# Zero-weight matmuls between the steps of a selective scan, and sums over states issued in odd units

## The chip, the cores and the metric

The kernel runs on one core of a Trainium2 chip. The metric is the device time of one execution in microseconds, and the time given is the median of the runs made. The engines of the core are named as in the profile: PE (TensorE), DVE (VectorE), ACT (ScalarE), POOL (GpSimd) and SP (SyncE, which here only issues DMAs).

## What is computed

Four layers work on 4 images of 64 x 64 positions with 128 channels. Layers 0 and 1 hold a two-dimensional selective scan; layer 2 is a gated message between neighbouring positions, layer 3 a 7 x 7 neighbourhood attention. The change lies in the scan of layers 0 and 1, whose core is, for each of four directions k, each inner channel d and each of 16 states n:

```python
def step(h, t):
    x_t, d_t, B_t, C_t = t
    h = jnp.exp(d_t[..., None] * A) * h + (d_t * x_t)[..., None] * B_t[:, :, None, :]
    return (h, jnp.einsum('bkdn,bkn->bkd', h, C_t))
_, ys_l = jax.lax.scan(step, h0, scan_in)
```

The scan runs over 4096 positions, along rows or along columns of the image, forwards or backwards. Around it stand projections, a 3 x 3 depthwise convolution, normalisations, gates and, in layer 1, an MLP. Layer 0 has 128 inner channels, layer 1 has 256.

## The kernel before

**Stages.** A short start; then one long scan stage for layers 0 and 1 together (about 200 to 11,487 us of the profiled span); then layers 2 and 3. The change touches the scan stage, and a constant at the start.

**Units.** A task is one image and one tile of 128 inner channels: 4 tasks in layer 0, 8 in layer 1. A task has 4 directions x 4 steps of 1024 positions x 16 units = 256 units, so there are 3072 units in all. A unit is 8 channels x 16 states on the 128 partitions, 1024 positions long. Two units make a pair, which shares one tile h.

**What a pair goes through.** A DMA on SP's queue brings delta times x into h, repeated over the states (`Scans.load`, L440), 10 units ahead. DVE multiplies both halves by B (`times`, L446). For each unit PE spreads delta over the states with two bf16 matmuls into a PSUM tile da (`decay`, L454), ACT turns da into exp(A delta) in place (L456), and DVE scans (`scan`, L465). da has two buffers, so the matmuls of unit u+2, issued in unit u, wait for the scan of unit u. ACT saves the last state (`save`, L483), POOL multiplies the pair by C (L446 again), and PE adds it over the states with four float32 matmuls into the PSUM tile yps (`add_up`, L547). Each float32 matmul shows as two records in the trace, so the sums of a pair are 8 records. yps is opened every 8 units by `sum_so_far` (L522 or L530, a matmul of the input or of the y of earlier directions) and copied out by ACT after 8 units (`keep`, L557). The tile h has 9 buffers; the load of pair p+9 waits for the sums of pair p.

**The order.** It is written out by hand in `Scans.run`: one turn of its loop is one unit, and each engine executes its instructions in the order in which the turns issue them. With v = u - LAG and LAG = 4, sums are issued in even units: those of pair p in unit 2p + 6. The order of a turn is: scan(u); in odd units the product with B; in even units save and the product with C; decay(u+2); add_up; keep; sum_so_far; then the pieces of other work; then load(u+10).

**The other work.** `prepare` (delta, B and C of later steps) and `Side` (everything else of layers 0 and 1) are generators cut into small pieces, each with a hint of the engines that it uses. Their recorded instructions stand under L97, since they go through the helper `Counted`. `Plan.slot` keeps an estimated time for PE, ACT and POOL, with 3.6 us for a unit, and is told how much of a unit's PE time the sums take: `1.6 * even`. A piece is issued in a unit if the estimate says that it fits. Its PE results go through one PSUM bank, ms. Its stores are posted and flushed to SP's queue later.

Of the kernel before, what the change touches and what calls it, by code (L numbers as in the profile page):

```python
# [10 lines left out]
BF16 = mybir.dt.bfloat16  # L11
# [6 lines left out]
P = 128  # L18
# [3 lines left out]
T = 512  # L22
# [22 lines left out]
class Consts:  # L45


    def __init__(self, tc, pool, d_gather, d_spread):
        nc = tc.nc

        gather = pool.tile([P, 56], F32, name="gather")
        nc.sync.dma_start(out=gather, in_=d_gather)
        self.gather = [gather[:, 24 - 8 * jj : 56 - 8 * jj] for jj in range(4)]

        self.spread = pool.tile([96, 4, P], BF16, name="spread")
        with tc.tile_pool(name="spread32", bufs=1) as tmp:
            spread = tmp.tile([96, 4, P], F32, name="spread32")
            nc.sync.dma_start(out=spread, in_=d_spread)
            nc.vector.tensor_copy(self.spread, spread)
        self.ident = pool.tile([P, P], F32, name="ident")  # L60
        make_identity(nc, self.ident)
        self.ones128 = pool.tile([P, P], F32, name="ones128")
        nc.vector.memset(self.ones128, 1.0 / 128.0)
        self.cen128 = pool.tile([P, P], F32, name="cen128")
        nc.vector.tensor_sub(self.cen128, self.ident, self.ones128)
        self.cen256 = pool.tile([P, P], F32, name="cen256")
        self.neg256 = pool.tile([P, P], F32, name="neg256")
        nc.vector.memset(self.neg256, -1.0 / 256.0)
        nc.vector.tensor_add(self.cen256, self.ident, self.neg256)
        self.eps = pool.tile([P, 1], F32, name="eps")  # L70
        nc.vector.memset(self.eps, EPS)
# [202 lines left out]
NU = ND * NSTEP * NG  # L274
AHEAD = 28
LEAD = 10
LAG = 4


class Scans:  # L280
# [253 lines left out]
    def add_up(self, p):  # L534

        hc = self.live.pop(("h", p))
        for v in range(2):
            t, step, jj, j, g = self.unit(2 * p + v)
            for i in range(HALVES):
# [6 lines left out]
                    out = out.rearrange("p (r l) -> p r l", l=ROWS)  # L546
                self.nc.tensor.matmul(out, self.C.gather[jj], rhs, start=False, stop=jj == 3)  # L547

    def keep(self, u):

        nc = self.nc
        t, step, jj, j, g = self.unit(u)
        k, c = t.steps[step]
        b = u % NG // 8
        if step == 0 and b == 0:
            t.y = self.pool.tile([P, L], F32, name="y", tag="y", bufs=1)
        nc.scalar.copy(self.part(t.y, k, c, b), self.like_part(self.live.pop("yps"), k))  # L557
        if step < len(t.steps) - 1:
            return
        for i in range(HALVES):  # L560
            for v in range(2):
                at, to = i * H + 32 * v, b * H + 32 * v
                src = t.y[at : at + 32, b * L // 2 : (b + 1) * L // 2].rearrange("p (a x) -> p a x", x=T)
                dst = t.yd[to : to + 32, :].rearrange("p (a i x) -> p a i x", i=HALVES, x=T)[:, :, i, :]
                self.later.append(lambda src=src, dst=dst: nc.sync.dma_start(out=dst, in_=src))

    def run(self, between):

        total = NU * len(self.tasks)
        first = self.tasks[0]  # L570
        first.W.load()
        for _ in self.fetch(first):
            pass
        for _ in self.prepare(first, 0):
            pass
        self.plan.start()
        pieces, fetch, fetched = Lane(self.plan, "prep", iter(())), iter(()), 0
        for u in range(-12, total + LAG + 1):
            v = u - LAG
            if 0 <= u < total:  # L580
                self.scan(u)
            if u % 2 and -1 <= u < total - 1:
                self.times(self.nc.vector, (u + 1) // 2, "B")
            if 0 < u <= total and u % 2 == 0:
                self.save(u // 2 - 1)
                self.times(self.nc.gpsimd, u // 2 - 1, "C")
            if 0 <= u + 2 < total:
                self.decay(u + 2)
                if (u + 2) % NG == 0:
                    self.bring_b(u + 2)  # L590
            if v > 0 and v % 2 == 0:
                self.add_up(v // 2 - 1)
            if v > 0 and v % 8 == 0:
                self.keep(v - 1)
            if 0 < v < total and v % 8 == 1:
                self.sum_so_far(v - 1)
            if u >= total:
                continue
            even, first_one = u % 2 == 0, u % NG == NG - 2
            self.plan.slot(  # L600
                u, 1.6 * even + 1.0 * (v % 8 == 1) + 2.0 * first_one, 0.25 * even + 0.7 * (v % 8 == 0)
            )
            ahead, rest = divmod(u + AHEAD, NG)
            if rest == 0:
                while pieces.step():
                    pass
                self.plan.flush("prep", "rep")
            if rest == 0 and 0 < ahead < total // NG:
                n, step = divmod(ahead, NU // NG)
                if step == 0 and self.tasks[n].W is not self.tasks[n - 1].W:  # L610
                    self.tasks[n].W.load()
                if step == 0 and fetched < n:
                    fetch, fetched = self.fetch(self.tasks[n]), n
                    for _ in range(self.tasks[n].W.nct):
                        next(fetch, None)
                pieces = Lane(self.plan, "prep", self.prepare(self.tasks[n], step))

            n, step = divmod(ahead + 1, NU // NG)
            if step == 0 and fetched < n < len(self.tasks) and self.tasks[n - 1].x_done:
                fetch, fetched = self.fetch(self.tasks[n]), n  # L620
            next(fetch, None)
            while (pieces.count < rest - 4 or pieces.fits()) and pieces.step():
                pass
            if u >= 0:
                n, i = divmod(u, NU)
                if self.later:
                    self.later.pop(0)()
                between(n, i)
            if 0 <= u + LEAD < total:
                self.load(u + LEAD)  # L630
        while self.later:
            self.later.pop(0)()
# [525 lines left out]
def scan_layers(tc, C, nb, x_in, d0, s0, d1, s1, out):  # L1158

    nc = tc.nc  # L1160
    with ExitStack() as es:
# [24 lines left out]
        def between(n, i):  # L1186
# [3 lines left out]

            done = group[n] - (1 if i >= 8 + LAG or n and group[n - 1] == group[n] else 2)
            left, rate = -(lane.count if lane else 0), 0.0
# [435 lines left out]
def layer2(tc, C, nb, x_in, x_out, d_w, d_rel, d_v, beside):  # L1628
    with ExitStack() as es:
# [11 lines left out]

        with tc.manual_schedule():
            run(statistics(0, range(8)))
            E.roots([E.rstd])
            run(project(0, range(4)))
            beside()

# [24 lines left out]
            third, second, last = halves[-3:]  # L1672
            gates = E.gates(out, last[2], [third[2]["var"]], [])
            run(merged(gates, E.finish(*third) + E.outputs(*second)))
            run(E.gather(*last, alone=True))
            E.roots([second[2]["var"]])
# [509 lines left out]
```

## Time and profile before

| | us |
|---|---|
| median of 3 runs (13,754.66 to 13,772.11) | 13,754.89 |
| the profiled execution | 13,747.0 |
| its span | 13,745.1 |
| busy in the span: PE / DVE / ACT / POOL | 9945.1 / 11,718.9 / 7914.9 / 9719.0 |
| granted TensorE clock, mean over the span | 0.744 |
| DMA moved | 2474.88 MB |

The page lists for each group of instructions its line, engine, operation, output and inputs with their shapes, its count, then busy time, mean length of one in ns, and the idle time of the engine just before with what ended it. A wait "A <- B" means that engine A stood idle at that line until B was done. In tables by stretch the columns are the busy time and count of PE, PEld (weight loads), DVE, ACT and POOL, then the granted clock as a share of full speed, the busy share of the DMA engines, and GB/s.

### The profile page before, as it was taken

How to read it: one execution, taken by the hardware profiler on the slowest of the kernel's cores; microseconds unless marked ns; L12 is line 12 of the kernel's file. 1: busy time of each engine (PE TensorE's matmuls, PEld its weight loads, DVE VectorE, ACT ScalarE, POOL GpSimd, SP SyncE). 2: the span in 40 equal slices, each digit the busy share in tenths (PEclk: the TensorE clock that was granted, in tenths of full speed). 3: DMA queues.
4: the chain of work that ended last, by engine and by line, in shares of the span. 5: the costliest groups of instructions: out<-in, count | busy, mean ns of one | idle time of the engine just before them, and what ended most of it. 6: DMA issues, size and time to landing. Idle time of an engine off the chain costs nothing. (4 is left out here: it accounts for less than half of the span.)

```text
span 13745.1 us, 120368 instructions
## 1 busy us (share of the span) xinstructions
PE 9945.1 (72%) x37178; PEld 2503.4 (18%) x37178; DVE 11718.9 (85%) x6980; ACT 7914.9 (58%) x10594; POOL 9719.0 (71%) x3218
## 2 busy tenths in 40 slices
PE   5777777777777777677776777777777766666688
PEld 1111111111111111111111111111111111111455
DVE  4998989989999889989999999999999993577555
ACT  3665556655665556555665555555555554655577
POOL 3777778877787778878887888888888884355200
PEclk7766766777677767767677777777777776778899
DMA  5878887898788878898889877878787873234300
GB/s 155 213 202 216 215 202 197 221 225 205 192 222 201 208 202 206 213 215 215 195 217 214 220 193 192 201 192 204 196 195 198 192 187 98 68 95 109 73 20 17
DMA packets 877051, 2474.88 MB, mean 180 GB/s; under 512 B 142456, under 2 KB 164096, under 8 KB 868216
## 3 DMA queue, kind: packets, MB, share of 16 engines
q1 hardware_dynamic: 876407, 2467.18, 72.6%
q8 instruction: 297, 4.87, 0.2%
q14 instruction: 347, 2.83, 0.1%
HBM read 2043.34 MB, written 272.37 MB: 168 GB/s over the span
## 5 line engine op out<-in xcount | busy, mean ns | idle before, releaser
L446 POOL TENSOR_TENSOR h<-h,repC 128x2048 f32<-128x2048 f32 x1536 | 6951.4, 4530 | 1708.5 <-ACT state L483 1370.7
L465 DVE TENSOR_TENSOR_SCAN h<-da,state,h 128x1024 f32<-128x1024 f32 x2304 | 5319.1, 2340 | 519.9 <-ACT da L456 401.5
L456 ACT ACTIVATE da<-da,av 128x1024 f32<-128x1024 f32 x3072 | 3338.7, 1088 | 3123.3 <-PE da L454 3106.0
L454 PE MATMUL da<-dp,spread 96*128 96x512 bf16 x6144 | 2481.8, 496 | 2302.3 <-DVE h L465 2275.6
L446 DVE TENSOR_TENSOR h<-h,B 128x2048 f32<-128x2048 f32 x1536 | 3476.9, 2264 | 363.7 <-DMA h<-dud 190.4
L547 PE MATMUL yps<-h,gather 128*32 128x512 f32 x12288 | 2424.3, 874 | 3.2 <-POOL h L446 3.2
L465 DVE TENSOR_TENSOR_SCAN h<-da,h 128x1024 f32<-128x1024 f32 x768 | 1727.6, 2281 | 160.8 <-ACT da L456 123.2
L454 PEld LDWEIGHTS <-spread 96*128 96x128 bf16 x6144 | 541.3, 107 | 5522.2 <-issue 5103.6
L97 PE MATMUL ms<-d,wts 128*128 128x512 f32 (+3 forms) x900 | 678.1, 878 | 213.2 <-POOL d L97 84.1
L97 ACT ACT_TABLE_LOAD x600 | 769.8, 1283 | 17.9 <-DMA h<-dud 2.6
L97 PE MATMUL ms<-xd,xpdt 8*128 8x512 f32 (+1 forms) x768 | 599.2, 870 | 220.7 <-ACT delta L97 71.9
L97 POOL TENSOR_TENSOR delta<-delta,low 128x1024 f32<-128x1024 f32 x192 | 452.3, 2356 | 382.0 <-ACT low L97 299.0
L1897 POOL COPY wide_total<-total 128x128 f32<-128x128 f32 x128 | 37.9, 296 | 830.1 <-DVE total L1895 642.7
L97 ACT CAST parts<-delta 128x1024 bf16<-128x1024 f32 x384 | 400.8, 1044 | 350.3 <-POOL delta L97 326.4
L530 PE MATMUL yps<-y,ident 128*128 128x512 f32 x576 | 508.2, 972 | 75.3 <-ACT y L557 73.3
L97 ACT ACTIVATE low<-ms,av 128x512 f32<-128x512 f32 x384 | 263.8, 687 | 451.0 <-PE ms L97 435.3
L97 POOL TENSOR_TENSOR low<-delta,xc 128x1024 f32<-128x1024 f32 x192 | 502.8, 2619 | 8.9
L547 PEld LDWEIGHTS yps<-h,gather 128*32 128x32 f32 x12288 | 281.7, 127 | 1089.4 <-issue 846.3
L97 PE MATMUL ms<-pad,diag 96*32 96x504 f32 (+1 forms) x2304 | 398.9, 801 | 108.8 <-DMA pad<-xid 80.5
L1453 ACT ACTIVATE hid<-hid,relb 128x1024 f32<-128x1024 f32 x288 | 322.8, 1146 | 265.8 <-DVE hid L1448 265.6
L1866 ACT ACTIVATE s<-s,least 128x512 f32<-128x512 f32 x512 | 372.3, 727 | 177.4 <-DVE least L1853 177.4
L1853 DVE CUSTOM_DVE_ANT_0 s<-sps,bias 128x512 f32<-128x512 f32 x512 | 323.3, 687 | 171.8 <-PE sps L1842 165.6
(284 smaller groups left out, 11039.2 us busy)
## 6 DMA issues: line engine op xcount, KB each, us to landing
h<-dud SPq DMA_DIRECT2D x3072, 512.0 KB
dp<-parts SPq DMA_DIRECT2D x2304, 64.0 KB
repC<-xdd SPq DMA_DIRECT2D x192, 512.0 KB
dud<-low SPq DMA_DIRECT2D x192, 512.0 KB
spread<-gd SPq DMA_DIRECT2D x72, 1024.0 KB
pad<-xid SPq DMA_DIRECT2D x192, 256.0 KB
szd<-o SPq DMA_DIRECT2D x96, 256.0 KB
xcd<-o SPq DMA_DIRECT2D x96, 256.0 KB
```

The costliest lines, as they stand in the source:

```text
L97: return call(*args, **kw)
L446: engine.tensor_mul(pair, pair, t.prepared[step][name].unsqueeze(1).to_broadcast([P, 2, TS]))
L454: self.nc.tensor.matmul(da[:, cols], self.C.spread[:, jj, :], dp[:, j, cols], start=True, stop=True)
L456: self.nc.scalar.activation(da, da, AF.Exp, scale=t.W.a[:, at : at + 1])
L465: nc.vector.tensor_tensor_scan(h[:, way], da[:, way], h[:, way], 0.0 if step % NSTEP == 0 else t.states[step - 1][:, u % NG : u % NG + 1], ...
L530: self.nc.tensor.matmul(self.like_part(yps, k), self.C.ident, self.part(t.y, k, c, b), start=True, stop=False)
L547: self.nc.tensor.matmul(out, self.C.gather[jj], rhs, start=False, stop=jj == 3)
L1453: nc.scalar.activation(hid, hid, AF.Gelu, bias=self.relb[:, m, t : t + 1])
L1853: self.nc.vector.tensor_tensor_reduce(out=self.live["s", n][:, h, :], in0=self.live["sps", n][:, h, :], in1=self.bias[case][:, h, :], scal ...
L1866: self.nc.scalar.activation(s, s, AF.Exp, scale=-1.0, bias=self.live["least", n][:, h : h + 1], accum_out=self.live["total", n][:, h : h + 1],
L1897: nc.gpsimd.tensor_copy(wide, total.unsqueeze(2).to_broadcast([P, self.NH, self.HD]))
```

## The change

`Consts` gets a 128 x 128 bf16 tile of zeros and a 128 x 512 bf16 tile of ones. At the end of each unit, after the other work's pieces and before load(u+10), two matmuls (even units) or three (odd units) multiply the ones by the zeros and add the result into the open yps; they are left out in the unit in which yps has just been copied out. LAG goes from 4 to 5, so that add_up, keep and sum_so_far are issued one unit later: the sums of pair p in unit 2p + 7. The plan is told the new place of the sums.

```diff
+        self.nothing = pool.tile([P, P], BF16, name="nothing")
+        nc.vector.memset(self.nothing, 0.0)
+        self.ones16 = pool.tile([P, T], BF16, name="ones16")
+        nc.vector.memset(self.ones16, 1.0)
...
-LAG = 4
+LAG = 5
...
+    def stay_busy(self, times):
+
+        for _ in range(times if "yps" in self.live else 0):
+            self.nc.tensor.matmul(
+                self.live["yps"], self.C.nothing, self.C.ones16, start=False, stop=False, skip_group_check=True
+            )
...
             self.plan.slot(
-                u, 1.6 * even + 1.0 * (v % 8 == 1) + 2.0 * first_one, 0.25 * even + 0.7 * (v % 8 == 0)
+                u, 1.6 * (not even) + 1.0 * (v % 8 == 1) + 2.0 * first_one, 0.25 * even + 0.7 * (v % 8 == 0)
             )
...
                 between(n, i)
+            self.stay_busy(3 if u % 2 else 2)
             if 0 <= u + LEAD < total:
                 self.load(u + LEAD)
```

## The prediction

> **What bounds the kernel now.** I began with the table of stages. The scan stage runs from 200 to 11,487 us, 82% of the span; columns are PE, PEld, DVE, ACT and POOL busy, granted clock, DMA share, GB/s.
>
> ```profile
> 200.00:11487.00 11287.00, 8218.74 (x26324) 1716.23 (x26328) 10418.23 (x4620) 6469.33 (x8005) 9062.68 (x2734) 0.72 0.83 204
> ```
>
> VectorE is busy 10,418 of 11,287 us (92%). PE is at 73% with a clock of only 0.72. Next the groups: all of VectorE's stage is scans and products with B.
>
> ```profile
> L465 DVE TENSOR_TENSOR_SCAN h<-da,state,h 128x1024 f32<-128x1024 f32 x2304 | 5319.1, 2340 | 519.9 <-ACT da L456 401.5
> L454 PE MATMUL da<-dp,spread 96*128 96x512 bf16 x6144 | 2481.8, 496 | 2302.3 <-DVE h L465 2275.6
> ```
>
> Then the waits: engine, line, what it waited for, total us, times, longest.
>
> ```profile
> PE da L454 <- DVE h L465: 2275.6, 1194, 10.6
> DVE h L465 <- ACT da L456: 524.7, 428, 10.4
> SPq L440 <- PE yps L547: 2652.2, 633, 11.5
> ```
>
> So VectorE loses 525 us waiting for exp(da), in 428 of 3072 units. That chain is: scan u-2 ends and frees the da bank, two matmuls on PE, one exp of 1.09 us on ACT, scan u. The timeline shows its room (PE rows, start, length):
>
> ```profile
> 5003.06 1.01 PE L454 MATMUL da<-dp,spread 96*128 96x512 bf16 x2 [3.56 <-DVE h L465]
> 5004.00 1.93 PE L547 MATMUL yps<-h,gather 128*32 128x512 f32 x8
> 5005.87 1.03 PE L454 MATMUL da<-dp,spread 96*128 96x512 bf16 x2
> 5009.81 1.01 PE L454 MATMUL da<-dp,spread 96*128 96x512 bf16 x2 [2.91 <-DVE h L465]
> ```
>
> VectorE's order is scan, scan, product B (2.34, 2.34, 2.26). So PE's da matmuls are released 2.3 us apart, then 4.6 us apart. Today the sums of y (1.93 us cold) sit in the short gap. The second da follows directly behind them, late; in the long gap PE idles 2.91 us. Between a bank's release and its next scan lie 4.6 us; 1.01 + 1.09 us of work and 0.2 of handing on leave 2.3 us of slack.
>
> Last, the clock. It is granted in windows of 3.41 us and is 0.50 or 1.00. Rows of such windows (length, PE busy, clock, DMA share, GB/s):
>
> ```profile
> 5027.90:5031.32 3.42, 3.42 (x10) 0.50 1.05 322
> 5031.32:5034.73 3.41, 2.74 (x15) 1.00 1.04 317
> 5034.73:5038.14 3.41, 1.57 (x8) 1.00 1.04 261
> 5038.14:5041.56 3.42, 0.62 (x2) 0.50 1.04 256
> 5041.56:5044.97 3.41, 3.07 (x11) 0.50 1.03 257
> 5044.97:5048.38 3.41, 2.54 (x6) 0.50 0.92 293
> ```
>
> A full cold window is followed by a warm one. A warm window at 80% keeps it, one at 46% loses it, and 90% of a cold window does not win it. I counted all 3306 windows of the stage so. Of 1453 warm ones, these stay warm: busy under 0.4, 0 of 346; 0.4 to 0.5, 4 of 126; 0.5 to 0.6, 84 of 138; 0.6 to 0.8, 296 of 396; above, 440 of 447; in all 57%. Of 1853 cold ones, these turn warm: under 0.8, 0 of 648; 0.8 to 0.9, 8 of 248; above, 621 of 957; in all 34%. In balance the warm share is 0.34/(0.34 + 0.43) = 0.44, clock 0.72, as the row says.
>
> **The change: fillers.** In the built program 6507 matmuls are added: two in even units, three in odd ones, none in the unit where the sum is copied out; 2.12 per unit. Nearest row: da, the same shape but 96 rows. A pair takes 0.60 us warm and 1.03 cold, one alone 0.38 and 0.6, so a further one is 0.215 warm and 0.43 cold. Their weight loads (0.1 us for da's) hide under the matmul before, as da's do; uncovered they would be 0.2 us of PE per unit. So a unit gets 0.46 us warm or 0.91 cold.
>
> What of it is hidden: PE idles 2276 us for scans, 0.74 us per unit, just where the fillers stand (directly ahead of the next da). A unit whose PE is on time pays nothing. A unit whose PE is late pays all of it, since da is queued behind. I followed each scan gap over 0.2 us back along its releasers. They sum to about 530 us; about 145 of them come through PE matmuls of the side work or the sums directly (some 220 us), about 180 through ACT, which had earlier waited for PE (some 218 us), and the rest from ACT, POOL or DMA. Bounds: 145 x 0.63 = +91 us, 325 x 0.63 = +205 us (0.63 at the clock worked out next). I take +91: in the second group the idle time often lies between.
>
> **The clock.** 0.46 us of 3.6 is +0.13 of a warm window, 0.91 of 3.68 is +0.25 of a cold one. Moving the counts by that much: warm windows of 0.3 to 0.4 (158) keep it in 0.1 of cases, 0.4 to 0.5 in 0.65, 0.5 to 0.6 in 0.75, 0.6 to 0.8 in 0.87, above as now: 16 + 82 + 104 + 345 + 440 = 987 of 1453, 68%. Cold windows above 0.7 (1353 in number with these at 0.7 to 0.8) become full, 70% of them turn; with 30 others 977 of 1853, 53%. Balance: 0.53/(0.53 + 0.32) = 0.62, clock 0.81; with the sums moved into the long gap I take 0.82 in the stage, 0.83 over the run (0.744 before).
>
> Here a rule of the Trainium skill is weighed (TensorE: Matmul & The Clock Gate, part 1, the clock gate): the clock falls after an idle window of about 3.4 us and comes after a busy one, so gaps under some 3 us are safe. By it, a PE with fillers in every gap would be warm nearly always, clock near 1. The rows above say otherwise: windows with 46% of work fall too, and 30% of even the full cold ones stay cold. The measurement decides: 0.82. The rule's end is a rival below.
>
> What is the clock worth? In the stage VectorE's busy time is its progress. By the table of 500 us stretches (same columns as the first row):
>
> ```profile
> 1000.00:1500.00 500.00, 372.62 (x1237) 70.83 (x1240) 443.96 (x198) 305.80 (x359) 379.12 (x119) 0.69 0.85 215
> 3500.00:4000.00 500.00, 362.65 (x1038) 74.94 (x1036) 456.36 (x202) 300.52 (x372) 402.40 (x120) 0.69 0.82 202
> 6000.00:6500.00 500.00, 380.94 (x1365) 72.72 (x1358) 458.27 (x204) 271.69 (x338) 397.89 (x119) 0.76 0.87 213
> 8000.00:8500.00 500.00, 362.98 (x1138) 80.69 (x1137) 475.82 (x212) 276.67 (x352) 425.96 (x129) 0.76 0.80 194
> ```
>
> The five full stretches at 0.69 average 457 us of VectorE, the twelve at 0.73 to 0.76 (mean 0.743) 464 us: 1.6% for 0.053. For +0.10 that is 3.0% of 11,287, 340 us. Cause runs both ways, since a stalled PE also cools. The lower bound is 0. I take two thirds, -227 us, because the direct working agrees: da (1.03 to 0.60), sums (1.93 to 1.07) and side matmuls (2.07 to 1.12) all lie in the late chains.
>
> **The sums moved.** They leave the short gap: da 1.03 + 1.93 there was already over 2.34, in the long gap it fits into 4.6. But the planner answers: side matmuls in even units rise from 1230 to 1809, in odd ones they fall from 1858 to 1279. That puts 0.38 of a matmul (0.4 to 0.8 us) per pair back. What remains is order: side results no longer stand behind the sums, so ACT gets them 1 to 2 us earlier. ACT-led gaps of odd units (151, 182 us) against even ones (27, 36 us) are the whole prize; I take a third of the excess, -50 us, bounds -145 and +50. The copy of y moves to the long gap too; with PE's wait for it (73 us) some -10.
>
> **SP.** A pair of h is freed one unit (3.7 us) later, and SP waits for that (third row of the waits). Behind it on SP's queue stand the stores and loads of the side work, dp, repC. VectorE's product starts 25 us (median; least 6.7) after its load is issued, so h itself stays covered. Side matmuls at PE's head waited 144 us in all for such loads (pad 54.8 and 35.1, xd 53.7). Bounds 0 and +144 doubled onto the path; I take +30, as only 34 of some 3088 side matmuls waited so. The two memsets lie beside the start's loads, and the one later unit at the stage's end costs at most 3.7 us: 0.
>
> **Sum.** -227 + 91 - 50 - 10 + 30 = -166 us. The profiled execution took 13,747.0 (span 13,745.1), the median of the runs is 13,754.9, 8 above it. So 13,755 - 166, about 13,590.
>
> **Rivals.** (1) As worked out, 0.55: 13,590, own range 13,440 to 13,700. (2) The skill's rule holds and PE stays warm, clock over 0.92: of the 525 us of waits and 69 more for B's matmuls some 420 go: 13,335; 0.17. For it: late layers show 0.98 at PE 89% busy. Against: SP and ACT stall PE for whole windows (346 under 0.4). (3) The clock rises, but VectorE's gaps are ACT's, POOL's and DMA's, or the fillers eat it: within 27 us; 0.11. (4) Slower: fillers with zero weights do not count as activity, or too little, and the clock stays at 0.72. Then a unit gets 2.12 x 0.334 = 0.71 us, PE goes from 2.68 to 3.39 of 3.67 us (92%), and 325 late units pay it in full: +230 + 30 - 60, 13,955. It decides if the stage's clock is under about 0.75; 0.17. In it the change does not do what it says.
>
> Faster 0.72, within 0.2% 0.11 (about what a measurement of this kernel can tell from no change), slower 0.17. The range, 13,310 to 13,850, leaves out less than half of (2) and most of (4).
>
> **What would show it.** Clock of the stage 0.80 to 0.86; VectorE's wait for exp(da) down from 525 to 300 to 400 us; PE's idle before da down from 2276 to under 1200; PE busy over 80%; SP's wait for the sums up. A stage clock under 0.75, or a wait for exp(da) over 600 us, would prove me wrong; so would waits of PE for side loads over 300 us.

## The result and the profile after

The changed kernel took 13,804.79 us (median of 6 runs, 13,795.66 to 13,812.74), the kernel before 13,754.77 in the same comparison: ratio 1.0036, 95% interval 1.0023 to 1.0049. It is 50 us slower where 165 us less was forecast. The time still lies inside the forecast's wide range of 13,310 to 13,850, but on the other side of the kernel before, so the range is no success of the reasoning. The profiled execution has a span of 13,797.4 us and a mean clock of 0.838.

Line numbers are now higher: da is L458, the exp L460, the scan L469, the sums L551, the added matmuls L556. First the scan stage in the table of stages, in the same stretch of time as before:

```profile
200.00:11487.00 11287.00, 8686.20 (x32116) 2277.83 (x32696) 10382.54 (x4600) 6469.76 (x7990) 9024.71 (x2726) 0.84 0.83 204
```

The granted clock went from 0.72 to 0.84, near the forecast (0.82). Yet in the same 11,287 us VectorE got through less: 10,382.54 us of work instead of 10,418.23, 20 instructions fewer. The groups and waits that answer to those shown before:

```profile
L469 DVE TENSOR_TENSOR_SCAN h<-da,state,h 128x1024 f32<-128x1024 f32 x2304 | 5316.1, 2340 | 587.9 <-ACT da L460 472.1
L458 PE MATMUL da<-dp,spread 96*128 96x512 bf16 x6144 | 2144.4, 435 | 1897.1 <-DVE h L469 1851.7
L556 PE MATMUL yps<-ones,nothing 128*128 128x512 bf16 x5934 | 1978.4, 427 | 96.2 <-issue 89.9
```

```profile
PE da L458 <- DVE h L469: 1851.7, 1363, 10.6
DVE h L469 <- ACT da L460: 601.0, 366, 15.1
SPq L444 <- PE yps L551: 3904.8, 893, 11.9
```

(The trace has 6516 weight loads of the added matmuls, 9 more than the prediction counted, but only 5934 of these matmuls: some records are missing, and PE's busy time is a little low.) da itself became faster (435 ns on average, 496 before) and PE idles 424 us less ahead of it. But VectorE's wait for exp(da), 525 us before, is 601: fewer waits, each longer (1.6 us instead of 1.2). The timeline shows what stands in them; PE's rows of one stretch:

```profile
5015.80 2.07 PE L101 MATMUL ms<-xd,xpdt 8*128 8x512 f32 x2
5017.80 1.46 PE L556 MATMUL yps<-ones,nothing 128*128 128x512 bf16 x3
5019.06 1.06 PE L458 MATMUL da<-dp,spread 96*128 96x512 bf16 x2
5020.05 1.97 PE L101 MATMUL ms<-d,wts 128*64 128x512 f32 x2
5021.95 1.03 PE L556 MATMUL yps<-ones,nothing 128*128 128x512 bf16 x2
5022.77 1.06 PE L458 MATMUL da<-dp,spread 96*128 96x512 bf16 x2
```

and VectorE's:

```profile
5015.16 2.29 DVE L469 TENSOR_TENSOR_SCAN h<-da,h 128x1024 f32<-128x1024 f32 x1 [2.57 <-ACT da L460]
5017.37 2.26 DVE L450 TENSOR_TENSOR h<-h,B 128x2048 f32<-128x2048 f32 x1
5021.27 2.29 DVE L469 TENSOR_TENSOR_SCAN h<-da,h 128x1024 f32<-128x1024 f32 x1 [1.65 <-ACT da L460]
5024.99 2.29 DVE L469 TENSOR_TENSOR_SCAN h<-da,h 128x1024 f32<-128x1024 f32 x1 [1.43 <-ACT da L460]
```

The da of 5022.77 belongs to an odd scan; its bank had been free since 5017.45. Ahead of it stand, in the short gap of the even unit, the even da, a side matmul (1.97 us cold) and two added ones: it starts 3.7 us after the even da, not 2.3, and VectorE waits 1.43 us. In this stretch the long gap overflows too: sums (1.94 us), a side matmul (2.07) and three added ones (1.46) stand ahead of the even da of 5019.06, and the even scan waits 1.65 us.

I sorted the scan gaps over 0.2 us of every trace by what ended them: PE-led where exp(da) waited for PE's matmuls, ACT-led where ACT had other work before exp(da). (The prediction's ACT-led gaps, 36 and 182 us, are only those in which ACT had itself waited for PE before; here all of them count.) Before: PE-led 68 us (even scans) and 155 (odd), ACT-led 76 and 222. After: PE-led 136 and 319, ACT-led 25 and 114. What ACT won, PE lost, and more. The sorting is a rule of thumb: where both came at nearly the same time a gap can go either way, which moves a sum by up to some 20 us.

### The profile page after: what moved, and what is told of

Same layout as the page of the kernel before. It is cut to its first block, busy times and chain, and to the rows that moved or that the text cites. A ratio compares the mean times of both kernels' runs of the same rounds, so it can differ in the third digit from the quotient of the medians.

```text
span 13797.4 us, 132709 instructions
## 1 busy us (share of the span) xinstructions
PE 10447.6 (76%) x43112; PEld 3074.1 (22%) x43694; DVE 11732.0 (85%) x6982; ACT 7932.1 (57%) x10594; POOL 9718.5 (70%) x3218
## 5 line engine op out<-in xcount | busy, mean ns | idle before, releaser
L469 DVE TENSOR_TENSOR_SCAN h<-da,state,h 128x1024 f32<-128x1024 f32 x2304 | 5316.1, 2340 | 587.9 <-ACT da L460 472.1
L460 ACT ACTIVATE da<-da,av 128x1024 f32<-128x1024 f32 x3072 | 3333.6, 1087 | 3382.5 <-PE da L458 3356.8
L458 PE MATMUL da<-dp,spread 96*128 96x512 bf16 x6144 | 2144.4, 435 | 1897.1 <-DVE h L469 1851.7
L556 PE MATMUL yps<-ones,nothing 128*128 128x512 bf16 x5934 | 1978.4, 427 | 96.2 <-issue 89.9
L551 PE MATMUL yps<-h,gather 128*32 128x512 f32 x12288 | 1933.4, 706 | 2.8 <-POOL h L450 2.8
L469 DVE TENSOR_TENSOR_SCAN h<-da,h 128x1024 f32<-128x1024 f32 x768 | 1727.6, 2280 | 167.9 <-ACT da L460 128.8
L458 PEld LDWEIGHTS <-spread 96*128 96x128 bf16 x6144 | 642.4, 106 | 3305.9 <-issue 2806.5
L556 PEld LDWEIGHTS <-nothing 128*128 128x128 bf16 x6516 | 552.5, 104 | 2380.0 <-issue 2148.3
L101 PE MATMUL ms<-d,wts 128*128 128x512 f32 (+3 forms) x900 | 563.9, 737 | 241.3 <-POOL d L101 132.5
L101 PE MATMUL ms<-xd,xpdt 8*128 8x512 f32 (+1 forms) x768 | 542.3, 792 | 107.1 <-DMA xd<-xdd 39.3
```

The costliest lines, as they stand in the source:

```text
L101: return call(*args, **kw)
L458: self.nc.tensor.matmul(da[:, cols], self.C.spread[:, jj, :], dp[:, j, cols], start=True, stop=True)
L460: self.nc.scalar.activation(da, da, AF.Exp, scale=t.W.a[:, at : at + 1])
L469: nc.vector.tensor_tensor_scan(h[:, way], da[:, way], h[:, way], 0.0 if step % NSTEP == 0 else t.states[step - 1][:, u % NG : u % NG + 1], ...
L556: self.nc.tensor.matmul(self.live["yps"], self.C.nothing, self.C.ones16, start=False, stop=False, skip_group_check=True)
```

## The experiments

**Theories at first.** F: the added matmuls stand ahead of da in late units, and that costs more than the clock brings. S: the shift frees h later, SP lags, PE stands at side matmuls without data. After the first four runs came P: the loss is the plan's answer, side matmuls moved into the short gap. Each run is given as a ratio to runs of the kernel before made beside it, with its 95% interval; 0.001 is 14 us. Differences between runs are taken from these ratios. The changed kernel itself is called the whole change. "Clock" is that of the scan stage, "wait" VectorE's wait for exp(da).

**Only the shift** (shift_only): the call of `stay_busy` is removed.

```diff
-            self.stay_busy(3 if u % 2 else 2)
```

> The change without its added matmuls: only the sums in odd units and the plan told so. Theory F (the added matmuls stand ahead of da in late units, and that price is larger than what the clock brings): this run is not slower than the kernel before, 13,650 to 13,755 us, clock of the run 0.72 to 0.76. Theory S (the loss comes from the shift: h is freed one unit later, SP's queue lags, and PE stands at side matmuls without data): this run is clearly slower than before and slower than the whole change, 13,850 to 14,000, with SP's wait for the sums near the 3900 us of the whole change.

Measured: 13,768.4 us, 1.0010 (1.0002 to 1.0018), clock 0.71, wait 538 us; SP's wait for the sums 3916 us. Slightly slower than before, which theory F had excluded (at most 13,755), but without most of the loss, against S too.

**Only the added matmuls** (fill_only): sums and plan as before.

```diff
-LAG = 5
+LAG = 4
...
-                u, 1.6 * (not even) + 1.0 * (v % 8 == 1) + 2.0 * first_one, 0.25 * even + 0.7 * (v % 8 == 0)
+                u, 1.6 * even + 1.0 * (v % 8 == 1) + 2.0 * first_one, 0.25 * even + 0.7 * (v % 8 == 0)
```

> The added matmuls alone, sums and plan as before (6900 or so matmuls, two in even units, three in odd ones). Theory F: slower than before, 13,850 to 13,950, since in even units sums, side matmuls and added ones all stand in the short gap; clock about 0.83. Theory S: faster than before, 13,500 to 13,650, at the same clock, SP's wait for the sums back near 2650 us.

Measured: 13,725.54 us, 0.9977 (0.9969 to 0.9986), clock 0.85, wait 519. Faster than before, where F had forecast a loss, but by far less than S had it (13,500 to 13,650). Each half alone costs or brings 0.1 to 0.2%, together they cost 0.36%. They do not add up, so something in their meeting was missing from both theories.

**Added only in quiet units** (fill_quiet), and **only in the others** (fill_busy, with `!=`):

```diff
+            booked = self.plan.at["PE"]
             ahead, rest = divmod(u + AHEAD, NG)
...
-            self.stay_busy(3 if u % 2 else 2)
+            if self.plan.at["PE"] == booked:
+                self.stay_busy(3 if u % 2 else 2)
```

> The whole change, but the matmuls are added only in units into which the plan put no side PE work. Theory F: the clock stays near 0.80 and the queue ahead of da is relieved in just the late units: 13,600 to 13,720, DVE's wait for exp(da) under 480 us. Theory S: the SP lag stays, so 13,780 to 13,830 as in the whole change.

> The complement of the run with the matmuls in quiet units: sums in odd units, and the matmuls added only in the units into which the plan did put side PE work (3121 instead of 3395, so nearly the same number). Theory F (price paid in units whose PE is late): 13,790 to 13,830, at least 60 us over the quiet placing, at a clock not lower than 0.77. If the price did not depend on the place: within 15 us of the quiet placing, 13,710 to 13,740.

Measured: quiet 0.9980 (0.9972 to 0.9988), clock 0.78, wait 495; busy 1.0056 (1.0042 to 1.0070), clock 0.77, wait 636. Nearly as many matmuls, the same clock, and 0.8% or 105 us between them: the price depends on the place, as F says, though F's ranges were missed by some 5 us each (13,725 for at most 13,720, 13,836 for at most 13,830), and the wait of the quiet placing was to be under 480.

**One per unit** (fill_one): `self.stay_busy(1)`.

> The whole change with one added matmul per unit instead of two or three (2700 or so instead of 6507). Theory F: clock about 0.78, half the price on the path: 13,720 to 13,780. Theory S: 13,790 to 13,850, since the clock's gain is smaller and the shift's loss the same.

Measured: 1.0000 (0.9992 to 1.0008), clock 0.77, wait 574. It lies in F's range.

**The quiet placing with sums and plan as before** (fill_only_quiet):

> Sums and plan as before the change, matmuls added only in units without side PE work (3459). Theory F: better than the kernel with all 6902 of them (13,725), 13,690 to 13,715, at a clock near 0.79; the best so far. If the clock itself is what counts: worse than that kernel, 13,735 to 13,750, since its clock is 0.06 lower.

Measured: 13,664.53 us, 0.9932 (0.9920 to 0.9944), clock 0.80, wait 469. Better than with twice as many and a clock of 0.85, and below F's range: the place counts more than the last 0.05 of clock. But the run shows a gain as well: nothing was added to the kernel before except these matmuls, which compute nothing that it needs, and it became 94 us faster while the clock rose from 0.72 to 0.80. In this order the clock, or the timing that comes with it, is worth at least that.

**SP relieved** (whole_lead9):

```diff
-LEAD = 10
+LEAD = 9
```

> The whole change, with the loads of h issued 9 units ahead instead of 10, so that a load stands as far behind the sums that free its tile as before the change, and what is queued behind it on SP is not held up by the shift. Theory S: SP's wait for the sums back to about 2700 us and the time to 13,740 to 13,770. Theories F and P: 13,790 to 13,820, PE's waits for DMAs hardly changed.

Measured: 1.0035 (1.0023 to 1.0048). SP's queue:

```profile
SPq L444 <- PE yps L551: 2889.8, 643, 11.8
```

The wait for the sums fell by a quarter, from 3905 us towards the 2652 of before, and the time did not move; nor did VectorE's own waits for loads of h (202 us, 192 with the whole change), so the later loads cost nothing that could hide a gain. Theory S falls. (A tenth buffer for h would be the more direct test; no run has it.)

**The plan told the old place** (whole_plan_old): the whole change, but for this line.

```diff
-                u, 1.6 * (not even) + 1.0 * (v % 8 == 1) + 2.0 * first_one, 0.25 * even + 0.7 * (v % 8 == 0)
+                u, 1.6 * even + 1.0 * (v % 8 == 1) + 2.0 * first_one, 0.25 * even + 0.7 * (v % 8 == 0)
```

> The whole change, but the plan is told that the sums are still in even units, so it puts side matmuls as before: 1153 in even units, 1935 in odd ones, instead of 1809 and 1279. Theory P (the loss that appears when shift and added matmuls come together is the plan's answer: side matmuls, which can stall at PE's head, move into the short gap ahead of the odd scans' da): 13,690 to 13,740, PE-led gaps of odd scans down from 318 to about 200 us. Theory F alone: 13,790 to 13,820, as the whole change, since as many matmuls stand in as many late units. Theory S: the same 13,800, since h is freed as late.

Measured: 13,571.83 us, 0.9864 (0.9851 to 0.9878): 0.0172 or 237 us under the whole change, and past P's range. This order, sums in odd units and the plan told that they are in even ones, is called the good order below. The waits of this kernel:

```profile
DVE h L469 <- ACT da L460: 390.0, 243, 12.5
SPq L444 <- PE yps L551: 3380.7, 836, 10.9
```

601 us of wait became 390. PE-led gaps of odd scans fell from 319 to 131 us, ACT-led ones from 114 to 69; those of even scans stayed (136 to 157, 25 to 29).

**The same without added matmuls** (shift_plan_old), and **the plan's line alone in the kernel before** (plan_alone):

> Sums in odd units, the plan told that they are in even ones, no added matmuls. Against the same kernel with all added matmuls (13,572) it prices these in the order that works. Theory P (place of the side matmuls is the main thing): 13,590 to 13,680, so still at least 80 us under the kernel before. If the added matmuls carry the gain: 13,700 to 13,760.

> The kernel before with one edit: the plan is told that the sums are in odd units, though they stay in even ones. Side matmuls in even units go from 1230 to 2116, in odd ones from 1858 to 972, so sums and most side matmuls stand together in the short gap. Theory P: 13,850 to 14,000, PE-led and ACT-led gaps of odd scans up by more than 100 us. If the place of side matmuls does not matter: 13,740 to 13,780.

Measured: shift_plan_old 13,596.57 us, 0.9884 (0.9871 to 0.9898), clock 0.72. The waits of shift_only, then of shift_plan_old:

```profile
DVE h L469 <- ACT da L460: 538.3, 397, 15.3
DVE h L469 <- ACT da L460: 373.0, 262, 11.8
SPq L444 <- PE yps L551: 3527.8, 852, 10.7
```

SP waits here nearly as long for the sums as with the whole change, and the kernel is 160 us faster than before, which speaks against S once more. plan_alone 13,860.68 us, 1.0079 (1.0067 to 1.0092), wait:

```profile
DVE h L465 <- ACT da L456: 653.6, 474, 12.8
```

with PE-led gaps of odd scans 310 us (155 before). Almost all of the gain in the good order is there without one added matmul. And moving 886 side matmuls into the short gap costs 0.8% in a kernel that is otherwise untouched. The place of the side work is thus shown as a cause, in both directions; P's mechanism, stalls at PE's head, is not (see below). ACT-led odd gaps rose in plan_alone only from 222 to 259, not by over 100 as expected. A piece of side work moves as a whole, with its work on ScalarE: 1844 of ScalarE's side instructions stand in even units in shift_only, 1566 in shift_plan_old. From shift_only to shift_plan_old ACT-led gaps of odd scans fall from some 214 to 82 us, PE-led ones from some 215 to 102. So what the plan's line is worth is the price of whole pieces, and not shown to be that of their matmuls alone.

**The quiet placing in the good order** (quiet_plan_old):

> The order that works (sums in odd units, plan as before), with added matmuls only in units without side PE work. Theory F: 13,520 to 13,565, under the 13,572 with all of them, as the quiet placing was better in both other orders (by 80 and 60 us). If in this order late units are few: within 15 us of 13,572.

Measured: 0.9872 (0.9857 to 0.9887), clock 0.79. No better than all of them, and outside F's range: F's price is small in this order.

**Further in the same direction** (plan_more: `3.6 * even`; plan_23: `2.3 * even`):

> The whole change with the plan told 3.6 us of sums in even units: side matmuls go further, 874 in even units and 2214 in odd ones (1153 and 1935 with 1.6). Theory P: 13,480 to 13,570. It ends where the long gap overflows: then 13,580 to 13,650, with gaps of even scans, which wait for what stands in odd units, up.

> The order that works with all added matmuls, the plan told 2.3 instead of 1.6 us of sums in even units: 1083 side matmuls there instead of 1153. A small step in the direction in which 3.6 starved the side work. Place theory: 70 matmuls less at 170 us per 656 is -18 us, 13,545 to 13,575. If the side work already falls behind: over 13,600.

Measured: 17,079.7 us, 1.2418 (1.2401 to 1.2435), and 1.0082 (1.0068 to 1.0096). The place theory missed both; for plan_23 the other case, side work that falls behind, came. In plan_more:

```profile
DVE h L469 <- ACT da L460: 3932.6, 109, 1256.7
```

The side work no longer fits, falls behind and is then issued in one go when the plan calls it late; VectorE stands for up to 1257 us. Eight such waits make up 3825 us; all other scan gaps, the shortest too, sum to 262 us. plan_23 has one of 118 us and PE-led odd gaps of 274. The 1.6 is near an edge.

**Time or stall?** Do side matmuls in the short gap hurt by the PE time that they take, or because they can stall at PE's head? To the good order with all added matmuls, three more are added in even units (even5: `3 if u % 2 else 5`) or in odd ones (odd6: `6 if u % 2 else 2`); they never stall (PE's idle time before them is 0.0 us in both).

> The order that works with all added matmuls (13,572), but five instead of two of them in even units. That puts 3 x 0.215 to 0.43 = 0.65 to 1.3 us of PE time into the short gap, as much or more than the 0.43 of a side matmul (0.5 to 0.9 us) per pair that the plan had moved there, and none of it can stall. If PE time in the short gap is the cause: 13,700 to 13,800. If stalls at PE's head are the cause: 13,570 to 13,630.

> The same kernel with six instead of three added matmuls in odd units, so the same PE time in the long gap. If gaps decide: at least 60 us cheaper than five in even units, 13,560 to 13,640. If added PE time costs the same anywhere: equal to the run with five in even units.

Measured: even5 0.9967 (0.9955 to 0.9980), clock 0.90, PE-led odd gaps 317 us. odd6 0.9861 (0.9847 to 0.9874), clock 0.89, PE-led odd gaps 115. Their waits, in this order:

```profile
DVE h L469 <- ACT da L460: 573.4, 431, 13.3
DVE h L469 <- ACT da L460: 410.4, 256, 12.6
```

Against 0.9864: plain PE time in the short gap costs 1.0%, 141 us for 4600 matmuls, 31 ns each; in the long gap 3450 cost nothing. Both figures are net of what the higher clock brought. The time taken is a sufficient cause; that stalls add to it is not excluded.

**Is the clock's gain hidden by the two in even units?** (odd3_only: `3 if u % 2 else 0`; odd6_only: `6 if u % 2 else 0`):

> The order that works, three added matmuls in odd units, none in even ones (3447 in all). If the two in even units cost 31 ns each as the further three there did (3064 x 31 ns = 95 us) and the clock carries a hidden gain: 13,470 to 13,520. If the two fitted into the short gap and the clock is worth little: 13,560 to 13,600, within 0.2% of the kernels with none (13,597) and with all (13,572).

> The same with six in odd units and none in even ones (6894). Clock as with all of the change's or higher. If the clock is worth something: below the run with three, by the hidden gain up to 13,450. If not: within 0.2% of it.

Measured: 0.9871 (0.9854 to 0.9888) at clock 0.80, and 0.9888 (0.9873 to 0.9903) at clock 0.85. Without any it was 0.9884 at 0.72. No gain comes out: the ratios do not fall as the clock rises. That does not make the clock worthless. PE-led gaps of odd scans fell to 76 and 69 us (some 102 without any), and those of even scans, ahead of which these matmuls stand, rose to 187 and 246 (100 without any). So a gain of the clock and a price of the matmuls in the long gap may cancel; no run raises the clock without adding matmuls.

**The runs side by side.** Ratios to the kernel before; the plan's line says where the plan is told that the sums are.

| sums in | plan told | none added | all | quiet units only |
|---|---|---|---|---|
| even units | even | 1 (before) | 0.9977 | 0.9932 |
| even units | odd | 1.0079 | no run | no run |
| odd units | odd | 1.0010 | 1.0036 (whole change) | 0.9980 |
| odd units | even | 0.9884 | 0.9864 | 0.9872 |

## Why the prediction was wrong, point by point

**The clock's height: right.** Stage 0.84 for 0.82 forecast, run 0.838 for 0.83. Of the 3.41 us windows 0.67 were warm (0.62 forecast). The 0.01 put on the moved sums did not come (0.71 in shift_only). The clock near 1 that the prediction had drawn from the Trainium skill (TensorE: Matmul & The Clock Gate, part 1) was rightly left to the measurement: of 170 warm windows at 0.4 to 0.5 only 31 stayed warm here too, and in odd6, whose trace lacks no added matmul, 4 of 125. Nor does it take a gap of 3 us: in the kernel before, 169 of the 175 warm windows at 0.4 to 0.6 that lost the clock had none that long, the longest being 1.7 us in the median.

**The added matmuls and their clock: the first failed step, -136 us (-227 for the clock, +91 for the matmuls).** Measured on top of the shift they cost 36 us (the whole change against shift_only), 172 us off. Without the shift they bring 32 (fill_only), in the good order 28 (whole_plan_old against shift_plan_old, within the intervals). How much of this is the clock's term and how much the matmuls' is not shown, since the clock was only ever raised by adding matmuls. What is shown of each:

The clock's -227 had no ground in the rows that it was read from. VectorE had 457 us in the stretches at 0.69 and 464 at 0.73 and above, but among the first it ranges from 444 to 473 and among the second from 439 to 476. Two of them, against the trend:

```profile
4500.00:5000.00 500.00, 375.49 (x1314) 73.81 (x1314) 438.96 (x195) 256.77 (x316) 370.77 (x110) 0.74 0.84 203
6500.00:7000.00 500.00, 367.44 (x1074) 75.96 (x1072) 473.00 (x211) 307.00 (x383) 418.64 (x126) 0.69 0.83 205
```

Over all 21 full stretches the correlation with the clock is 0.3, with the place in the stage 0.7. What raising the clock brings depends on the order: net of the matmuls, 94 us for 0.08 in the order before (fill_only_quiet), 41 us for 0.07 on the shift (fill_quiet against shift_only), and between a loss of 6 us and a gain of 32 for 0.07 to 0.17 in the good order, where none, odd3_only, quiet_plan_old, whole_plan_old, odd6_only and odd6 (clock 0.72, 0.80, 0.79, 0.85, 0.85, 0.89) have 0.9884, 0.9871, 0.9872, 0.9864, 0.9888, 0.9861.

The matmuls' +91 had the right mechanism (late units pay), but no gap in it: a further matmul costs 31 ns in the short gap and nothing in the long one, each net of its clock. It was also too low, by an estimate: on the shift the quiet placing brings 41 us and the busy one costs 63 at nearly the same clock, so if the clock is worth as much in both, 3121 matmuls in busy units alone cost 104 us or more.

What was forecast for the wait (300 to 400 us), for PE's idle time before da (under 1200) and for PE's busy share of the stage (over 80%) failed with it: 601, 1852 and 77% (78% in whole_lead9, whose trace has all 6516 added matmuls). The wait just passed the 600 us that the prediction had named as a sign of being wrong.

**The sums moved: the second failed step, -60 us with the plan's answer in it.** The prediction had the right rows, the short gap and the 1230 side matmuls that become 1809, and then let the two cancel but for a third of ACT's gaps. Measured one by one: the shift with the side matmuls nearly in place (1153 in even units) brings 160 us (shift_plan_old), the plan's answer takes 173 back (shift_only against it). It nets +14 us (shift_only), not -60.

So the sum that holds is -160 + 173 + 36 = +49 us, and 50 were measured. The steps are not independent: with all matmuls added the plan's answer costs 237 us instead of 173, and then the sum reads -160 - 28 + 237. This is why the one line decides the sign. With it held still the change takes 13,572 us, within 20 of the forecast 13,590, but by luck: the shift brings 160 where 60 was forecast, and the matmuls 28 where 136 was.

**SP, +30 us**, did not come: relief of its wait by 1000 us changed nothing, and PE's waits for side loads (pad 82.7 and 38.4, xd 39.3 us) hardly rose from 144. (The trace before gives 31 us as the median between the issue of a load of h and its product, not 25; the least, 6.7, is right.) **Rival 4** gave the right sign, but not its mechanism: the clock did not stay at 0.72; rival 3 had named the fillers' eating the gain.

Left open: what the clock alone is worth; and how much of a side piece's harm in the short gap is its PE time, how much a stall, and how much its work on ScalarE.

## What to carry to other kernels

Where one engine's steps are released in an uneven rhythm, work on a queue ahead of them is priced by the gap that it stands in, not by its sum: the 2.3 us gap was full, the 4.6 us gap had room. When a change moves a step that a planner knows of, the planner's answer is part of the change; cost every instruction that it moves, or hold it still and measure both. A difference between stretches of one trace is no price for the clock: set it first against the scatter among stretches of the same clock, and remember that work added to raise the clock has a price of its own, so a run with it gives only the net.

## What was not expected of the hardware

PE's clock could be raised from 0.72 to 0.89 of full speed by multiplying with zeros, and a kernel in which PE is 73% busy gained 0.2% (shift_plan_old and odd6): PE's matmuls were short enough where they had room. da's mean fell from 499 to 415 ns and the sums' from 834 to 661 ns; the rows of da in these two runs:

```profile
L458 PE MATMUL da<-dp,spread 96*128 96x512 bf16 x6140 | 2489.6, 499 | 2393.5 <-DVE h L469 2353.5 <-DMA h<-dud 16.8 <-DMA dp<-parts 7.7
L458 PE MATMUL da<-dp,spread 96*128 96x512 bf16 x6140 | 2031.3, 415 | 1510.9 <-DVE h L469 1461.2 <-DMA dud<-low 11.7 <-DMA dp<-parts 10.1
```

In the order before, where da is often late, a rise to 0.80 came with 0.7% (fill_only_quiet). Of 511 cold windows that were full in the changed kernel 342 turned warm and 169 did not, so even a full window does not always bring the clock.
